# Activations in place, one squaring instruction and six early gate heads in a planned attention kernel

## The chip, the cores and the metric

The kernel runs on one core of a Trainium2 chip. Its time is the device time of one execution in microseconds (us); lower is better. The core has five engines that run their own queues in order and meet at semaphores: TensorE (PE, matrix products; its weight loads are listed as PEld), VectorE (DVE), ScalarE (ACT), GpSimd (POOL) and SyncE (SP), which here issues nearly all DMA transfers.

## The reference

The model has two layers over 4 x 256 tokens of 256 channels, all in float32: a conditioning stage, an attention, a second conditioning stage and a mixture of experts, twice. Only the attention of the first layer is touched:

```python
conv = silu(causal_conv_4_taps(x @ w_qkv))
q, k, v = split(conv)                 # 16 heads of q and k, 32 of v, 128 wide
core = chunk_gated_delta_rule(l2norm(q), l2norm(k), v, g, beta)
out = core * rsqrt(mean(core * core) + EPS) * norm_w
out = out * silu(x @ w_z)
return out @ w_out
```

The delta rule needs, for each chunk of tokens, the products of keys with keys and of keys with queries (the Gram blocks), the inverse of a unit triangular matrix made of them, and with it the new values and the outputs.

## The kernel before, in words

**Tiling.** The tokens are cut into two halves (`s` = 0, 1) of two sequences `b` of 256 tokens. One *unit* is one key head of one half, with its two value heads: 16 units in each half, 32 in all. A unit holds its 256 tokens as two chunks `n` of 128. Four units form a `Group` (line 447), which shares the inversion of the 32 x 32 diagonal blocks on VectorE (`small_inverses`, line 482: 30 steps of a multiply and a subtract, plus 32 x 32 transposes). `Rest` (line 1797) holds the other stages of a half: experts, a gated mix, and eight more experts.

**A planner sets the order.** Every step is declared as an `op` (line 194) with an engine, a cost and the buffers it reads and writes. `Tape.plan` (line 289) places the steps one by one, by how late each may start and when its engine, its buffers and its inputs are free; the constants of line 418 weigh this. It plans ten times, takes the plan that it holds for the shortest, and emits the steps in that order, which is then each engine's queue. So a change to one step's cost, to a buffer count or to a constant can move steps in every queue. All of them are issued through one wrapper, so nearly everything in the profile carries line 128, and groups are told apart by tile names.

**Places.** Every tile of 512 elements in a partition takes one of `PLACES` = 59 common places (`place`, line 1443). `MOST` caps how many places one use may hold at a time (4 if not named), and `RATE` and `FEW` keep some free for more urgent steps.

**Around the change, in one unit.** `products` (line 771) loads `wqk` and makes `acck_k` and `accq_q` (`convolved`, line 728: two products on PE, a scaled copy on ACT, three taps on DVE). ACT takes the Silu of each half of each, into `kq[0]` and `kq[1]`, which hold chunk `n` of keys (`j` = 0) and queries (`j` = 1) side by side. `gram` (line 795) multiplies a chunk's keys with the keys and queries of a chunk in one matmul of 256 columns per sequence. ACT squares each `kq` into `sq`, and `norms` (line 851) sums the squares on PE into `ps_kt`; small steps on DVE and POOL make the scales of them. POOL and ACT build the decay matrices `attnT`. `values`, `inverse` and `outputs` follow and leave the outputs in `vo[0]` and `vo[1]`. `normed` (line 1277) takes the sum of squares of each row of `vo` into `rs`: four ACT instructions for each chunk, each with an accumulator that a further instruction reads out. POOL adds an epsilon, takes the power -1/2, and scales `vo` by `rs` and by the gate `zs`; PE turns it into `oT` and `project` (line 658) multiplies by `wo`.

**Early gates.** `gates` (line 1213) is the product `x @ w_z` and its Silu: 8 float32 matmuls of 256 columns for each of two chunks. For units named in `EARLY` (line 421), which are two (heads 3 and 4 of half 0), it is declared ahead of all groups (`early`, line 1260), kept in DRAM, and loaded back when `normed` needs it. Each float32 matmul is two MATMUL instructions in the profile, each with a weight load.

Of the kernel before, what the change touches and what calls it, by code (L numbers as in the profile page):

```python
# [414 lines left out]
            o.emit()  # L415


ROUNDS, SWITCH, LOAD, SPARE, AHEAD, EACH, END, IDLE, MOMENT, GAP, RATE, GIVES = 10, 11.7, 1.3, 106.8, 160.0, 23.99, 1300.0, 54.95, 0.68, 66.3, 3.14, 5.0
UNIT = 42

EARLY, FEW = range(3, 5), 6
WIDE = 96
WINDOW, ENOUGH, LITTLE, SLOW, THIN = 3.4, 0.51, 0.38, 0.5, 10.0

# [260 lines left out]
class Unit:  # L685
# [85 lines left out]
    def products(self):  # L771
# [2 lines left out]
        gate = p.gateb[s]  # L774
        w = self.load("wqk")

        kq = self.kq = [self.buf([P, 2, 2, P], "kq0", 2), self.buf([P, 2, 2, P], "kq1", 6)]
        for j, at in ((1, 0), (0, 1)):
            acc = self.convolved(w, at, at * NH + h, "qk"[j == 0])
            for n in range(2):  # L780

                def emit(n=n, j=j, acc=acc):
                    e.scalar.activation(
                        kq[n]()[:, :, j, :], acc()[:, :, n * P : n * P + P], AF.Silu
                    )

                op("ACT", _act(256), emit, [acc], [(kq[n], {j})], table="silu")


        kqm = []  # L790
# [3 lines left out]
        cost = lambda n: (engine, length(n))  # L794
        def gram(n0, n, ps):
            for b in range(2):
                e.tensor.matmul(
                    ps()[:, b * 256 : b * 256 + 256],
                    kq[n0]()[:, b, 0, :],
                    kq[n]()[:, b].rearrange("p j d -> p (j d)"),  # L800
                    start=True,
                    stop=True,
                )

        for pairs in (((0, 0),), ((1, 1), (0, 1))):
# [11 lines left out]
            op(  # L817
                "PE",
                _mm(256, 2 * len(of)),
                grams,  # L820
                kq[: len(of)],
                [ps for _, _, ps, _ in of],
                to=[m for _, _, _, m in of],
            )
# [12 lines left out]
        sums = lambda j: ps()[:, 504 + 4 * j : 508 + 4 * j]  # L837

        sqs = []
        for n in range(2):  # L840
            sq = self.buf([P, 2, 2, P], "sq", 2, name=n)
            sqs.append(sq)
            op(
                "ACT",
                _act(512),
                lambda n=n, sq=sq: e.scalar.activation(sq(), kq[n](), AF.Square),
                [kq[n]],
                [sq],
            )

        def norms(ps=ps):


            for at in reversed(range(8)):
                j, n, b = at // 4, at // 2 % 2, at % 2
                e.tensor.matmul(
                    ps()[:, 505 + at - WIDE : 505 + at],
                    sqs[n]()[:, b, j, :],
                    p.const(LT)[:, P - WIDE :],
                    start=True,  # L860
                    stop=True,
                )
# [414 lines left out]
    def normed(self):  # L1277


        p = self.p  # L1280
        e, op = p.e, p.tape.op
        vo, zs = self.vo, self.zs
        tt = e.gpsimd.tensor_tensor
        junk = self.buf([P, P], "junko", 1)
        rs = self.buf([P, 2, 2, 2], "rs", 3)

        def o(n):
            return vo[n]().rearrange("p v b d -> p (v b) d")

        def roots(n):  # L1290
            return rs()[:, n].rearrange("p v b -> p (v b)")

        for n in range(2):

            def squares(n=n):
                for q in range(4):
                    e.scalar.activation(
                        junk(), o(n)[:, q, :], AF.Square, accum_out=roots(n)[:, q : q + 1]
                    )

            op("ACT", 1.95, squares, [vo[n]], [junk, (rs, {n})])

        def shifted():
            eps = self.eo().rearrange("p (n b) -> p n b", n=2)
            tt(rs(), rs(), _over(eps, 2, 2), ALU.add)

        def root():
            flat = rs().rearrange("p n v b -> p (n v b)")
            tt(flat, flat, p.neghalf, ALU.pow)

        op("POOL", 0.22, shifted, [self.eo], [rs])
        op("POOL", 1.64, root, [], [rs])
# [17 lines left out]
        self.oT = []  # L1330
        for v in range(2):
            oT = self.buf([P, 512], "oT", 4, name=v)
            self.oT.append(oT)
            ps = p.ps(f"ot{v}_{self.tag}")

            def turn(v=v, ps=ps):
                for b in range(2):
                    for n in range(2):
                        at = (2 * b + n) * P
                        e.tensor.transpose(  # L1340
                            ps()[:, at : at + P], vo[n]()[:, v, b, :], p.const(IDENT)
                        )
# [12 lines left out]
class Program:  # L1355
# [80 lines left out]
            return self.place(tag, name, shape)  # L1436
        return Buf(self.tape, pool, shape, tag, f"{tag}_{name}", bufs)

    PLACES = 59

    MOST = {'attnT': 20, 'kq1': 12, 'kq0': 2, 'kqm': 16, 'cross': 10, 'vo': 8, 'zs': 6, 'oT': 6, 'w0': 6, 'hw0': 8, 'w1': 6, 'hw1': 8, 'wo': 2, 'sq': 4, 'r0': 5, 'wqk': 20, 'vn': 20, 'acck': 20, 'wb0': 12}

    def place(self, use, name, shape=(P, 512)):

# [772 lines left out]
```

## Time and profile before

| what | value |
|---|---|
| median of 3 runs (lowest, highest) | 1481.29 us (1479.42, 1482.24) |
| the profiled execution's own time | 1474.44 us |
| its span, first to last instruction | 1472.6 us |
| mean granted PE clock | 0.981 of full |
| places, cap of `wqk`, `vo`, `wo`, `wb0` | 59, 20, 8, 2, 12 |
| MATMUL instructions of the early gates | 32 |
| DMA, mean rate | 87 GB/s |

The profile is of one execution. In its engine rows a percentage is busy time over the span. A row of a group has the engine, the operation, the tiles (output, then inputs), the shape, the count, then busy time in us and the mean ns of one instruction, and last the idle time of its engine just before it with what ended that. Matmuls overlap: the mean of a MATMUL is its latency from start to end, and what one costs in a row of many is the distance from start to start, which the timeline shows. In a table of stages each engine has its busy us and, in brackets, its instructions; PEclk is the granted clock.

### The profile page before, as it was taken

Reading aid. Unit: us, or ns where it says so; the run is one execution under the profiler, and the core shown is the slowest. Engines: PE = TensorE matmul, PEld = TensorE weight load, DVE = VectorE, ACT = ScalarE, POOL = GpSimd, SP = SyncE. Lnnn points to the kernel's source line nnn. Section 1 sums busy time; section 2 is a strip of 40 time slices with the busy share of each in tenths; the row PEclk is TensorE's granted clock in tenths of the full one; section 3 lists DMA queues with packets and bytes.
Section 4 is the critical chain, followed back from the end, with each engine's and each line's share of the span. In section 5 each row is a group of like instructions: output and inputs, shape, how many; then the busy total and the mean of one; then the engine's idle time right before and its main releaser. Section 6 shows DMA issues by size and latency. Waiting matters only on the chain.

```text
span 1472.6 us, 24086 instructions
## 1 busy us (share of the span) xinstructions
PE 1388.6 (94%) x8428; PEld 899.4 (61%) x8428; DVE 1127.7 (77%) x2117; ACT 932.7 (63%) x2013; POOL 918.6 (62%) x913
## 2 busy tenths in 40 slices
PE   4987899999999899999999999889999999999988
PEld 2655676876875686776687677654445644444433
DVE  7799898798698679889879989955785677785133
ACT  2688788888878888888888887733342742121220
POOL 3069859948754785985986875448643654664032
PEclk9998999999999899999999999999999999999999
DMA  6042122211120231222231223155332231658030
GB/s 213 10 136 76 47 77 87 83 46 41 59 73 29 74 98 62 66 73 72 66 110 50 65 54 94 44 165 157 107 105 83 73 126 55 188 155 245 0 115 14
DMA packets 80953, 128.60 MB, mean 87 GB/s; under 512 B 10160, under 2 KB 26288, under 8 KB 80832
## 3 DMA queue, kind: packets, MB, share of 16 engines
q1 hardware_dynamic: 79824, 125.91, 28.0%
q8 instruction: 67, 1.10, 0.3%
q10 hardware_dynamic: 1008, 1.16, 0.3%
q14 instruction: 54, 0.44, 0.1%
HBM read 121.36 MB, written 5.67 MB: 86 GB/s over the span
## 4 chain that ended last, share of the span: by engine, by line
PE 70%; DVE 15%; POOL 5%; ACT 4%; issue 3%; DMA 2%; SPq 0%; DVEq 0%; POOLq 0%; ACTq 0%
PE ps_wo L128 7%; PE ps_cvv L128 6%; PE ps_h L128 5%; PE ps_a L128 5%; PE ps_z L128 5%; PE ps_at L128 4%; PE ps_gram L128 4%; PE ps_ae L128 4%; PE ps_e L128 3%; PE ps_kt L128 3%; PE ps_cvk L128 3%; PE ps_cvq L128 3%; PE ps_vn L128 3%; DVE accv_v L128 2%; PE ps_mix L128 2%
## 5 line engine op out<-in xcount | busy, mean ns | idle before, releaser
L128 ACT ACT_TABLE_LOAD x114 | 146.3, 1283 | 21.5 <-DVE sb_xT L128 8.9
L128 DVE SCALAR_TENSOR_TENSOR accv_v<-ps_cvv,sb_convw,accv_v 128x510 f32<-128x510 f32 (+2 forms) x192 | 141.7, 742 | 7.2 <-ACT accv_v L128 2.2
L128 POOL TENSOR_TENSOR hw_h<-hw_h,r_h 128x512 f32<-128x512 f32 x64 | 85.9, 1348 | 77.7 <-DVE hw_h L128 76.1
L128 PE MATMUL ps_cvv<-ratio,wv 128*128 128x512 f32 x256 | 122.5, 609 | 2.3 <-DVE acck_k L128 1.3
L128 PE MATMUL ps_h<-ratio,w_w 128*128 128x512 f32 x256 | 117.7, 601 | 7.4 <-DMA w_w<-in_w 5.8
L128 ACT ACTIVATE r_h<-ps_h 128x512 f32<-128x512 f32 x64 | 38.2, 597 | 132.2 <-PE ps_h L128 129.4
L128 PE MATMUL ps_a<-hw_h,w_w 128*128 128x512 f32 x256 | 117.0, 595 | 1.6 <-POOL hw_h L128 1.6
L128 PE MATMUL ps_z<-wz,ratio 128*128 128x256 f32 x480 | 116.1, 390 | 0.4 <-ACT zs L128 0.4
L128 PE MATMUL ps_wo<-oT,wo 128*128 128x512 f32 x256 | 112.8, 593 | 0.8 <-ACT oT L128 0.8
L128 POOL TENSOR_TENSOR hw_e<-hw_e,r_e 128x512 f32<-128x512 f32 x32 | 41.5, 1312 | 92.1 <-ACT r_e L128 61.0
L128 PEld LDWEIGHTS ps_z<-wz,ratio 128*128 128x128 f32 x480 | 89.8, 194 | 14.2 <-issue 0.9
L128 POOL TENSOR_TENSOR vd<-vn,dc 128x512 f32<-128x512 f32 x32 | 34.1, 1064 | 98.3 <-ACT vn L128 97.8
L128 POOL TENSOR_TENSOR X<-attnT,kqm 128x512 f32<-128x512 f32 x64 | 83.6, 1314 | 12.4 <-ACT kqm L128 12.1
L128 PEld LDWEIGHTS ps_h<-ratio,w_w 128*128 128x128 f32 x256 | 48.5, 192 | 67.2 <-issue 59.8
L128 DVE TENSOR_TENSOR xs<-xs,prod 128x30 f32<-128x30 f32 (+14 forms) x240 | 81.2, 338 | 8.2
L128 PEld LDWEIGHTS ps_a<-hw_h,w_w 128*128 128x128 f32 x256 | 48.0, 190 | 61.5 <-issue 51.6
L128 ACT ACTIVATE junko<-vo 128x128 f32<-128x128 f32 x256 | 79.4, 310 | 7.3
L128 PEld LDWEIGHTS ps_wo<-oT,wo 128*128 128x128 f32 x256 | 48.1, 190 | 58.7 <-issue 53.1
L128 DVE TENSOR_TENSOR prod<-xs,Rt 128x30 f32<-128x30 f32 (+14 forms) x240 | 78.8, 328 | 6.4
L128 POOL TENSOR_TENSOR attnT<-attnT,kqm 128x512 f32<-128x512 f32 x64 | 82.6, 1303 | 1.5
L128 DVE SCALAR_TENSOR_TENSOR hw_h<-ps_h,wb_wb 128x512 f32<-128x512 f32 x64 | 43.8, 684 | 51.8 <-ACT r_h L128 39.2
L128 PE MATMUL ps_at<-vn,attnT 128*128 128x128 f32 x512 | 82.1, 276 | 0.0
(258 smaller groups left out, 3764.1 us busy)
## 6 DMA issues: line engine op xcount, KB each, us to landing
attnT<-G SPq DMA_DIRECT2D x64, 256.0 KB, 4.9
w_w<-in_w SPq DMA_DIRECT2D x64, 256.0 KB, 4.4
wb_wb<-w_rows SPq DMA_DIRECT2D x128, 128.0 KB, 3.3
wqk<-in_wqk SPq DMA_DIRECT2D x32, 256.0 KB, 2.9
wv<-in_wv SPq DMA_DIRECT2D x32, 256.0 KB, 3.6
wo<-in_wo SPq DMA_DIRECT2D x32, 256.0 KB, 3.0
qe<-G SPq DMA_DIRECT2D x32, 256.0 KB, 3.6
wz<-in_wz SPq DMA_DIRECT2D x30, 256.0 KB, 2.7
```

The source lines that it names most:

```text
L128: return self._tc.keep_in_program_order(f(*a, **k))
```

## The change

Four things are edited, and the constants with them.

1. **Keys and queries in place.** The Silu of a unit's keys is one ACT instruction over 512 elements, written over `acck_k`; that of the queries likewise over `accq_q`. The tiles `kq0` and `kq1` are gone, so the `acc` tiles live until the last Gram block and square. Keys and queries no longer lie side by side, so each Gram matmul of 256 columns becomes two of 128. The squares are taken for keys and for queries instead of for chunk 0 and chunk 1.
2. **Output squares of the second chunk.** ACT squares all of `vo[1]` in one instruction into a new tile `osq` (one place), and VectorE sums it with one `tensor_reduce`. The first chunk stays as it was.
3. **Early gates for six units.** `EARLY` is heads 2 to 7 instead of 3 and 4.
4. **Places and caps.** 61 places; `vo` 16, `wo` 6, `wqk` 8, `wb0` 3 and `wb1` 8 (it had the 4 of a use not named). Two weights of the planner move a little (`SPARE`, `IDLE`).

```diff
-ROUNDS, SWITCH, LOAD, SPARE, AHEAD, EACH, END, IDLE, MOMENT, GAP, RATE, GIVES = 10, 11.7, 1.3, 106.8, 160.0, 23.99, 1300.0, 54.95, 0.68, 66.3, 3.14, 5.0
+ROUNDS, SWITCH, LOAD, SPARE, AHEAD, EACH, END, IDLE, MOMENT, GAP, RATE, GIVES = 10, 11.7, 1.3, 102.83, 160.0, 23.99, 1300.0, 57.77, 0.68, 66.3, 3.14, 5.0
...
-EARLY, FEW = range(3, 5), 6
+EARLY, FEW = range(2, 8), 6
...
-        kq = self.kq = [self.buf([P, 2, 2, P], "kq0", 2), self.buf([P, 2, 2, P], "kq1", 6)]
+        kq = [None, None]
         for j, at in ((1, 0), (0, 1)):
-            acc = self.convolved(w, at, at * NH + h, "qk"[j == 0])
-            for n in range(2):
-
-                def emit(n=n, j=j, acc=acc):
-                    e.scalar.activation(
-                        kq[n]()[:, :, j, :], acc()[:, :, n * P : n * P + P], AF.Silu
-                    )
-
-                op("ACT", _act(256), emit, [acc], [(kq[n], {j})], table="silu")
+            acc = kq[j] = self.convolved(w, at, at * NH + h, "qk"[j == 0])
+            op(
+                "ACT",
+                _act(512),
+                lambda acc=acc: e.scalar.activation(acc(), acc(), AF.Silu),
+                [],
+                [acc],
+                table="silu",
+            )
+
+        def chunk(j, n, b):
+            return kq[j]()[:, b, n * P : n * P + P]
...
-                e.tensor.matmul(
-                    ps()[:, b * 256 : b * 256 + 256],
-                    kq[n0]()[:, b, 0, :],
-                    kq[n]()[:, b].rearrange("p j d -> p (j d)"),
-                    start=True,
-                    stop=True,
-                )
+                for j in range(2):
+                    at = (2 * b + j) * P
+                    e.tensor.matmul(
+                        ps()[:, at : at + P],
+                        chunk(0, n0, b),
+                        chunk(j, n, b),
+                        start=True,
+                        stop=True,
+                    )
...
-        for n in range(2):
-            sq = self.buf([P, 2, 2, P], "sq", 2, name=n)
+        for j in range(2):
+            sq = self.buf([P, 2, T], "sq", 2, name=j)
...
-        for n in range(2):
-
-            def squares(n=n):
-                for q in range(4):
-                    e.scalar.activation(
-                        junk(), o(n)[:, q, :], AF.Square, accum_out=roots(n)[:, q : q + 1]
-                    )
-
-            op("ACT", 1.95, squares, [vo[n]], [junk, (rs, {n})])
+        def squares():
+            for q in range(4):
+                e.scalar.activation(
+                    junk(), o(0)[:, q, :], AF.Square, accum_out=roots(0)[:, q : q + 1]
+                )
+
+        op("ACT", 1.95, squares, [vo[0]], [junk, (rs, {0})])
+        squared = self.buf([P, 4, P], "osq", 1)
+        op(
+            "ACT",
+            _act(512),
+            lambda: e.scalar.activation(squared(), o(1), AF.Square),
+            [vo[1]],
+            [squared],
+        )
+        op(
+            "DVE",
+            _dve(512),
+            lambda: e.vector.tensor_reduce(roots(1), squared(), AX.X, ALU.add),
+            [squared],
+            [(rs, {1})],
+        )
...
-    PLACES = 59
+    PLACES = 61
...
-'vo': 8, 'wo': 2, 'wqk': 20, 'wb0': 12
+'vo': 16, 'wo': 6, 'wqk': 8, 'wb0': 3, 'wb1': 8
```

The last two lines are cut to the entries that differ.

More of the change, by code (lines that the diff above doesn't have):

```diff
@@ L818, in products @@
                 "PE",
-                _mm(256, 2 * len(of)),
+                _mm(128, 4 * len(of)),
                 grams,
-                kq[: len(of)],
+                kq,
                 [ps for _, _, ps, _ in of],
@@ L845, in products @@
                 _act(512),
-                lambda n=n, sq=sq: e.scalar.activation(sq(), kq[n](), AF.Square),
-                [kq[n]],
+                lambda j=j, sq=sq: e.scalar.activation(sq(), kq[j](), AF.Square),
+                [kq[j]],
                 [sq],
@@ L857, in norms @@
                     ps()[:, 505 + at - WIDE : 505 + at],
-                    sqs[n]()[:, b, j, :],
+                    sqs[j]()[:, b, n * P : n * P + P],
                     p.const(LT)[:, P - WIDE :],
@@ L1437, in buf @@
         return Buf(self.tape, pool, shape, tag, f"{tag}_{name}", bufs)
-    PLACES = 59
-    MOST = {'attnT': 20, 'kq1': 12, 'kq0': 2, 'kqm': 16, 'cross': 10, 'vo': 8, 'zs': 6, 'oT': 6, 'w0': 6, 'hw0': 8, 'w1': 6, 'hw1': 8, 'wo': 2, 'sq': 4, 'r0': 5, 'wqk': 20, 'vn': 20, 'acck': 20, 'wb0': 12}
+    PLACES = 61
+    MOST = {'attnT': 20, 'kq1': 12, 'kq0': 2, 'kqm': 16, 'cross': 10, 'vo': 16, 'zs': 6, 'oT': 6, 'w0': 6, 'hw0': 8, 'w1': 6, 'hw1': 8, 'wo': 6, 'sq': 4, 'r0': 5, 'wqk': 8, 'vn': 20, 'acck': 20, 'wb0': 3, 'wb1': 8}
     def place(self, use, name, shape=(P, 512)):
```

## The prediction, made before the changed kernel was run

> **What bounds the kernel now.** I read the page's engine rows first, then its slices, then the chain of work that ended last:
>
> ```profile
> PE 1388.6 (94%) x8428; PEld 899.4 (61%) x8428; DVE 1127.7 (77%) x2117; ACT 932.7 (63%) x2013; POOL 918.6 (62%) x913
> ...
> PE   4987899999999899999999999889999999999988
> ...
> DVE  7799898798698679889879989955785677785133
> ...
> PE 70%; DVE 15%; POOL 5%; ACT 4%; issue 3%; DMA 2%; SPq 0%; DVEq 0%; POOLq 0%; ACTq 0%
> ```
>
> PE is busy 94% of the span and holds 70% of the chain, so PE sets the time, except where its row falls under 9. ACT, from which the change takes most, is third and holds 4%. The table of stages (start:end, length, then busy us by engine) shows where PE falls short:
>
> ```profile
> 40.00:100.00 60.00, 57.71 (x232) 37.16 (x232) 51.46 (x111) 46.53 (x86) 18.50 (x20) 0.98 0.27 89
> 100.00:200.00 100.00, 80.31 (x718) 63.45 (x717) 90.68 (x175) 83.42 (x176) 89.93 (x89) 0.90 0.19 58
> 200.00:900.00 700.00, 686.80 (x5438) 507.79 (x5437) 594.63 (x1119) 592.41 (x1355) 519.73 (x519) 0.99 0.23 68
> ```
>
> From 40 to 200 us PE idles 2.3 + 19.7 = 22.0 us, and from 100 to 200 at a clock of 0.90, so about 8 of its 80.3 busy us there are slowness. From 200 to 900 it idles 13.2 us of 700. In the chain the stretch from 98 to 186 us is almost all DVE and ACT (taps, transposes and the 30 steps of the first inversions): there PE has nothing urgent. The list of PE's waits from 80 to 200 us names the holes:
>
> ```profile
> PE ps_kt L128 <- ACT sq L128: 8.0, 1, 8.0
> PE ps_lu L128 <- DVE vo L128: 6.5, 1, 6.5
> PE ps_z L128 <- DVE eo L128: 2.5, 1, 2.5
> ```
>
> **The change part by part.** *Early gates.* These can move PE work out of the PE-bound stretch into those holes. The stages of tile `ps_z` alone (PE first) give what stands there now:
>
> ```profile
> 40.00:100.00 60.00, 3.81 (x16) 2.89 (x16) 1.19 (x2) 0.98 0.27 89
> 100.00:200.00 100.00, 18.30 (x64) 13.87 (x64) 4.63 (x8) 0.90 0.19 58
> ```
>
> 80 instructions, at 16 a unit, are five units before 200 us (two early, three in turn). With six early heads and heads 0 and 1 in turn there can be eight: three more, 48 instructions. At the start-to-start distance of a matmul of 256 columns, 0.215 us (below), that is 10.3 us, and 22.0 us of holes can hold it. The ends are 0 (the holes stand in PE's in-order queue before one late instruction, and the planner may still put nothing into them) and 10.3. I take 10.3, since a gate needs only the activations and a weight, both there from 40 us. A fuller PE should also hold its clock: ends 0 and 8 us, and I take 2, as the deepest hole's cause stays. The early Silu calls on ACT (0.6 us, two a unit) move with the gates into a stretch where ACT is busy 83% and on the chain; six of them cost up to 3.6 us there, and the in-place Silu gives back 0.39 us a unit (below) for the first eight units, 3.1: even. On SP and the DMA queue four more units mean four weight loads sooner, eight stores and eight reloads of 256 KB; a store's issue took 0.32 us, so 16 of them 5.1 us over several hundred, landing in 2.1 to 2.6 us. Four loads at the start, at the 241 GB/s of the first 20 us, could hold up the first inputs by 4.4 us; I take 0, since the loads of before (12.3 us) already stood behind them.
>
> *Gram blocks.* Three adjacent lines of PE's timeline (start, us, ...) price both shapes:
>
> ```profile
> 116.67 1.03 PE L128 MATMUL ps_gram<-kq 128*128 128x256 f32 x4
> 117.53 1.04 PE L128 MATMUL ps_vt<-sb_consts,accv_v 128*128 128x128 f32 x8
> 118.41 1.89 PE L128 MATMUL ps_z<-wz,ratio 128*128 128x256 f32 x8
> ```
>
> Four instructions of 256 columns took 117.53 - 116.67 = 0.86 us, 0.215 each; eight of 128, each with its own weights, 0.88, 0.110 each. A block of four becomes eight: +0.02 us, three a unit, 32 units: +1.9 us of PE. A rule speaks against this split: the Trainium skill, "TensorE: Matmul & The Clock Gate", Back-to-back issue gap, says that in a stream of weight load and matmul pairs the spacing is set by both, about 81 ns at 128 columns and 131 at 512. On a straight line between, 256 columns are 98 ns, and two of 128 cost 162/98 = 1.65 times as much. On the 12 x 0.215 = 2.58 us of Gram blocks a unit that would be +1.7 us, +54 us in all, and the change would end near 1525. The row is of this kernel's type, shape and weight loads, so the row decides; 54 us stays as the far end, given little weight.
>
> *Silu in place, and the squares.* The groups (busy us, mean ns):
>
> ```profile
> L128 ACT ACTIVATE junko<-vo 128x128 f32<-128x128 f32 x256 | 79.4, 310 | 7.3
> L128 ACT ACTIVATION_READ_ACCUMULATOR junko<-vo 128x1 f32 x256 | 48.1, 188 | 0.0
> L128 ACT ACTIVATE sq<-kq 128x512 f32<-128x512 f32 x64 | 37.8, 622 | 0.3
> L128 ACT ACTIVATE kq<-acck_k 128x256 f32<-128x256 f32 x64 | 24.1, 409 | 0.8 <-DVE k L128 0.7
> L128 ACT ACTIVATE accv_v<-accv_v 128x512 f32<-128x512 f32 x64 | 38.6, 626 | 1.2 <-DVE accv_v L128 0.8
> ```
>
> Silu: four of 0.41 us become two of 0.626, -0.39 us a unit, -12.5 us of ACT. Squares of the second chunk: four pairs of 0.310 + 0.188 = 1.99 us become one of 0.622, -1.37 a unit, -43.8 us. ACT falls by 56 us to about 876. PE's listed waits on ACT from 200 to 950 us add up to only some 6 us, so I put this at 0 (at most 6).
>
> *The sum on VectorE.* The nearest rows are small reductions:
>
> ```profile
> L128 DVE TENSOR_REDUCE r_route<-r_rk 128x32 f32<-128x256 f32 x2 | 0.8, 420 | 0.1
> L128 DVE TENSOR_REDUCE r_route<-r_route 128x4 f32<-128x32 f32 x4 | 0.7, 186 | 0.1
> ```
>
> (420 - 186)/224 = 1.045 ns an element, so 512 take 420 + 256 x 1.045 = 0.69 us; 32 of them 22.0 us of DVE, to 1150. Its cover is DVE's 105 us of idle from 200 to 900, which takes 27 or so of the units, 18.6 us: DVE goes from 85% to 88%. With the cover gone all 22 us would count. There is a new wait: the sum sits in DVE's queue until ACT has squared. Behind it wait the taps of later heads, whose PSUM banks PE needs. The planner orders both, so I take 0 and keep 0.5 us a unit, 16 us, as the far end. Below nothing is possible too: the pair takes 0.62 + 0.69 us where ACT alone took 1.99, so `rs` is ready some 0.5 us sooner; POOL's waits for it (44.6 us, "rs <- ACT junko") are of an engine off the path, so nothing is counted. Whether the sum also collides with POOL is open: the skill's "SBUF — State Buffer", SBUF: two separate sides, says that VectorE shuts GpSimd out of a shared port pair in a two-port mode or with two SBUF inputs, and "VectorE: DVE Perf Modes" that a `tensor_reduce` runs only in the plain mode. By the rule no collision; no run here shows it, and the rows fit, without excluding a blocked one. If it blocked, a wait of up to one POOL product (1.28 us) each would be 41 us of DVE.
>
> *Places and caps.* No `kq` tiles means two places fewer a unit held for as long as the Gram blocks wait; `osq` takes one and the pool gains two. That lets values and gates run further ahead: 0 to -10 us (half of PE's 13.2 us of idle from 200 to 900, and of the 7 us that a clock of 0.99 costs there), taken at 0. `wb0` falls to 3: the products of one expert (8 instructions of 0.43 us) take 3.4 us, and a row of weights lands 3.3 us after issue, so two in hand are enough: 0, or up to the 11.3 us that DVE waits for such rows now, once more.
>
> **The sum.** -10.3 (gates) - 2 (clock) + 1.9 (Gram) = -10.4 us, against the profiled execution's 1474.4 us: 1464.0. The median of the runs shown is 6.9 us higher, at 1481.3, so on it I forecast 1471.
>
> **Rivals.**
>
> 1. *VectorE becomes the pace from 200 to 900 us.* For it: DVE is busy 9 tenths in many slices there, holds 15% of the chain, and gets 22 us and a wait more. Against: PE's waits on DVE there are each under 2 us. If all of the 22 us land before steps that PE needs: 1481.3 - 10.3 + 1.9 + 22.0 = 1495. It decides from 8.4 us on, some 0.26 us a unit, where the gain is used up.
> 2. *The gates are only shuffled.* The holes stay, or the critical steps near 120 us slip by as much: 1481.3 + 1.9 = 1483. For it: the planner could fill these holes before with gates of heads 0 to 4 and left 22 us open. Against: four heads now stand free that waited behind their group.
> 3. *The plan gets looser everywhere*, thanks to places and a freer ACT: 1471 - 10 = 1461. For it: fewer tiles held; against: only 13 us of idle to win.
>
> **How the numbers follow.** 42% for the forecast (1464 to 1478), 15% for rival 3, 13% for rival 2, 30% for rival 1 and its like (any new order that keeps PE waiting). 0.2% is 3.0 us, about what a measurement of this kernel can tell from no change. Faster by more: 42 + 15 + 1 = 58%; within: 12%; slower: 30%. The range takes in rival 3 with 9 us to spare and ends at rival 1: 1452 to 1495.
>
> **What would show it.** Right: some 128 `ps_z` instructions before 200 us and less PE idle from 100 to 200 with a clock over 0.90; Gram rows of 128 columns, 768 in all, about 0.110 us apart; ACT near 876 us; DVE near 1150 with 32 sums of 0.69 us; PE idle from 200 to 900 still near 13 us. Wrong: as many gates as before by 200 us, sums longer than 0.8 us, DVE's share of the chain well over 15%, or PE waiting for DVE in that stretch. What would upset all of it is the order itself: a new plan in the first 200 us that starts the PE-bound stretch later than 186 us.

## The result, and the profile after

| | before | after |
|---|---|---|
| median of 5 runs each (lowest, highest), us | 1482.24 (1479.42, 1483.47) | 1495.0 (1492.25, 1496.02) |
| span of the profiled execution, us | 1472.6 | 1494.1 |
| mean granted PE clock | 0.981 | 0.974 |
| PE idle in the span, us | 84.0 | 92.2 |

The ratio is 1.0079, interval 1.0062 to 1.0096: the change costs 12.8 us where a gain of 10 was forecast. The profiles lie 21.5 us apart, more than the medians, since the profiled execution of before, 1474.4 us, was one of its quickest (of 134 timed runs of before on record two took 1474.5 us or less); why it was is part of what follows.

The page of the changed kernel, its engine rows, the slices of PE and DVE, and the shares of the chain of waits:

```profile
PE 1401.9 (94%) x8812; PEld 921.3 (62%) x8812; DVE 1151.6 (77%) x2149; ACT 922.1 (62%) x1744; POOL 913.3 (61%) x913
...
PE   3998799999999899999999999899999998999988
...
DVE  7799899799699779889889879875686686674133
...
PE 71%; DVE 12%; POOL 6%; ACT 4%; DMA 3%; issue 3%; SPq 1%; ACTq 0%; DVEq 0%; POOLq 0%
```

DVE's share of the chain fell from 15% to 12% while its busy time rose by 23.9 us, so VectorE did not become the pace. PE is busy 13.3 us longer: as estimates, 2 are the Gram blocks, and a clock of 0.974 instead of 0.981 makes 1401.9 x 0.007 = 10 of the rest. PE also idles 8.2 us more. The table of stages (start:end, length, busy us and instructions of PE, PEld, DVE, ACT, POOL, then PE's clock, DMA share, GB/s):

```profile
40.00:100.00 60.00, 55.90 (x265) 38.18 (x265) 50.02 (x96) 42.12 (x70) 18.58 (x23) 0.96 0.29 101
100.00:200.00 100.00, 82.45 (x699) 63.24 (x698) 90.24 (x170) 71.39 (x139) 79.60 (x79) 0.87 0.22 66
200.00:900.00 700.00, 687.62 (x5706) 521.07 (x5705) 602.97 (x1142) 589.53 (x1162) 515.77 (x515) 0.99 0.24 73
```

From 200 to 900 us PE idles 12.4 us, 13.2 before: nothing is lost there inside the stretch. From 40 to 200 it idles 21.6, 22.0 before: the holes are as large as they were, and the clock fell from 0.90 to 0.87. Of tile `ps_z` alone the same view has

```profile
40.00:100.00 60.00, 7.62 (x32) 5.78 (x32) 2.39 (x4) 0.96 0.29 101
100.00:200.00 100.00, 17.77 (x64) 13.68 (x64) 4.64 (x8) 0.87 0.22 66
```

96 gate instructions by 200 us; 80 before, 128 forecast. (A unit has four float32 matmuls of gates for each chunk, not the eight that the part on early gates gives; 16 instructions a unit are right.) What became late is the first group. The 32 x 32 transposes that open and close its small inverses (tiles `Rt` and `Tc`) start at 126.1 and 157.9 us, against 118.4 and 149.8 before. The rows of `Tc` give shortest, median and longest duration in ns, then the starts of the first group's and the last group's, before and after:

```profile
L128 DVE STREAM_TRANSPOSE Tc<-xs x8: 1934/1984/1993, 149.8 to 930.3; 128x1024 f32<-128x1024 f32 x8
```

```profile
L128 DVE STREAM_TRANSPOSE Tc<-xs x8: 1920/1988/1998, 157.9 to 938.6; 128x1024 f32<-128x1024 f32 x8
```

So some 8 us are lost before 160 us and are still missing at 940; the other 13 of the two spans' difference are lost after that. PE's stretch from the last `Tc` to the end, before and after:

```profile
930.27:1472.60 542.33, 515.70 (x1816) 255.40 (x1814) 334.40 (x592) 178.96 (x335) 262.18 (x257) 0.99 0.36 111
```

```profile
938.62:1494.10 555.48, 519.90 (x1812) 256.88 (x1810) 343.87 (x609) 183.40 (x308) 273.45 (x269) 0.98 0.36 105
```

With as many instructions left, PE idles 35.6 us there instead of 26.6.

The groups of the edited steps (busy us, mean ns, then idle before):

```profile
L128 ACT ACT_TABLE_LOAD x133 | 170.6, 1283 | 21.0 <-DVE ek L128 9.8 <-PE ps_z L128 4.0 <-DVE sb_xT L128 3.6
L128 ACT ACTIVATE junko<-vo 128x128 f32<-128x128 f32 x128 | 39.6, 310 | 3.8
L128 ACT ACTIVATION_READ_ACCUMULATOR junko<-vo 128x1 f32 x128 | 23.9, 187 | 0.0
L128 ACT ACTIVATE osq<-vo 128x512 f32<-128x512 f32 x32 | 20.2, 632 | 2.9 <-POOL attnT L128 2.0
L128 ACT ACTIVATE acck_k<-acck_k 128x512 f32<-128x512 f32 x32 | 20.0, 625 | 1.6 <-DVE acck_k L128 1.4
...
L128 DVE TENSOR_REDUCE rs<-osq 128x4 f32<-128x512 f32 x32 | 21.6, 676 | 5.5 <-ACT osq L128 5.4
```

Every price of the prediction is there: squares and their read-outs halved (79.4 to 39.6 and 48.1 to 23.9), sums of 0.676 us. But ACT fell by 10.6 us only, not 56. Its groups without table loads fall by 48, the new order switches ScalarE's function tables (Silu and the exponential, for instance, lie in different ones) 19 times more (114 to 133 loads of 1.283 us, +24 us), and the rest is overlap of neighbouring instructions, which busy time counts once: the groups sum to 68 us more than the busy time before, and to 55 after.

### The profile page after: what moved, and what is told of

The parts are those of the page before. It is cut to its first block, busy times and chain, and to the rows that moved or that the text cites. A ratio compares the mean times of both kernels' runs of the same rounds, so it can differ in the third digit from the quotient of the medians.

```text
span 1494.1 us, 24638 instructions
## 1 busy us (share of the span) xinstructions
PE 1401.9 (94%) x8812; PEld 921.3 (62%) x8812; DVE 1151.6 (77%) x2149; ACT 922.1 (62%) x1744; POOL 913.3 (61%) x913
## 4 chain that ended last, share of the span: by engine, by line
PE 71%; DVE 12%; POOL 6%; ACT 4%; DMA 3%; issue 3%; SPq 1%; ACTq 0%; DVEq 0%; POOLq 0%
PE ps_wo L128 6%; PE ps_cvv L128 6%; PE ps_z L128 6%; PE ps_h L128 5%; PE ps_at L128 5%; PE ps_a L128 5%; PE ps_gram L128 4%; PE ps_kt L128 4%; PE ps_cvq L128 3%; PE ps_vn L128 3%; PE ps_ae L128 3%; PE ps_cvk L128 3%; PE ps_e L128 2%; DMA w_w<-in_w 2%; PE ps_lx L128 2%
## 5 line engine op out<-in xcount | busy, mean ns | idle before, releaser
L128 PE MATMUL ps_z<-wz,ratio 128*128 128x256 f32 x416 | 99.9, 386 | 0.7 <-ACT kqm L128 0.7
L128 PEld LDWEIGHTS ps_z<-wz,ratio 128*128 128x128 f32 x416 | 76.3, 191 | 13.5 <-issue 2.2
L128 DVE SCALAR_TENSOR_TENSOR hw_h<-ps_h,wb_wb 128x512 f32<-128x512 f32 x64 | 43.8, 687 | 50.4 <-ACT r_h L128 47.2
L128 POOL TENSOR_TENSOR vo<-vo,zs 128x512 f32<-128x512 f32 x64 | 82.3, 1306 | 0.0
```

The source lines that it names most:

```text
L128: return self._tc.keep_in_program_order(f(*a, **k))
```

## The experiments

Two kinds of kernel are needed to tell prices from order. In a kernel with a **fixed order** only what a step emits is edited, not the cost or buffers that the planner sees, so that every queue stays as it was but for the edited instructions. A kernel **planned anew** has the edit declared, and the whole order may move. Ratios are to the kernel before, run beside each on the same chip. Three chips were used, and before's own median beside these runs lay between 1482.3 and 1486.2 us, so rows are compared by their ratios and not by their medians; a difference of 0.2 to 0.3% between two rows is about what their intervals can tell.

| run | kernel, edits | order | median us | ratio (interval) |
|---|---|---|---|---|
| after | the change | new | 1495.0 | 1.0079 (1.0062, 1.0096) |
| e2 | after, old squares | after's | 1491.43 | 1.0051 (1.0031, 1.0072) |
| e7 | after, mask | after's | 1491.9 | 1.0040 (1.0022, 1.0057) |
| e13 | after, mask, old squares | after's | 1486.48 | 1.0012 (1.0002, 1.0022) |
| e1 | before, Gram, sum late | before's | 1508.6 | 1.0176 (1.0146, 1.0205) |
| e6 | before, mask | before's | 1475.84 | 0.9938 (0.9917, 0.9959) |
| e8 | before, mask, Gram, sum late | before's | 1492.99 | 1.0064 (1.0041, 1.0086) |
| e9 | before, mask, Gram | before's | 1475.72 | 0.9948 (0.9928, 0.9968) |
| e10 | before, mask, sum late | before's | 1497.16 | 1.0090 (1.0065, 1.0116) |
| e11 | before, mask, sum early | before's | 1483.43 | 0.9999 (0.9984, 1.0013) |
| e3 | after, two early heads | new | 1489.89 | 1.0047 (1.0027, 1.0067) |
| e4 | before, six early heads | new | 1492.16 | 1.0061 (1.0042, 1.0081) |
| e12 | before, mask, six early heads | new | 1485.01 | 1.0018 (1.0000, 1.0037) |
| e14 | after, mask, two early heads | new | 1487.81 | 1.0023 (1.0008, 1.0038) |
| e15 | before, mask, new places and caps | new | 1502.29 | 1.0120 (1.0102, 1.0137) |
| e16 | after, mask, old places and caps | new | 1505.47 | 1.0155 (1.0128, 1.0183) |
| e17 | after, mask, old cap of `wb0`, `wb1` | new | 1498.62 | 1.0106 (1.0078, 1.0133) |
| e18 | before, mask, Silu in place, Gram | new | 1496.51 | 1.0094 (1.0068, 1.0120) |

**e1, the new operations in the old order.** Gram split, squares of the second chunk in one instruction, their sum on VectorE at the head of POOL's step `shifted`.

```diff
+                if n == 1:
+                    e.scalar.activation(self.osq, o(1), AF.Square)
+                    return
...
         def shifted():
+            e.vector.tensor_reduce(roots(1), self.osq, AX.X, ALU.add)
...
-                    kq[n]()[:, b].rearrange("p j d -> p (j d)"),
+                        kq[n]()[:, b, j, :],
```

> Keeps the old order of every queue and puts only two of the change's operations into it: Gram matmuls of 128 columns, and the second chunk's squares as one ACT instruction with their sum on VectorE, emitted just ahead of POOL's use. Order theory (the loss of 13 us comes from the new order, not from what the operations cost): within 4 us of before, since Gram adds about 2 us of PE and the sums lie beside other work. Operation theory (the 22 us of sums, or the doubled matmuls, set the pace): 8 to 22 us slower than before, and PE waits on VectorE from 200 to 900 us grow by as much.

1508.6 us, 1.0176: more than the whole change loses. So operations that were counted at +1.9 us in sum cost 26 in an order not made for them; e8 below parts this into what is theirs and what is not.

**e2, the old squares in the new order.** Accumulators on ACT as before, no sum; the step for the sum emits nothing.

```diff
-            lambda: e.scalar.activation(squared(), o(1), AF.Square),
+            lambda: [
+                e.scalar.activation(squared()[:, q, :], o(1)[:, q, :], AF.Square, accum_out=roots(1)[:, q : q + 1])
+                for q in range(4)
+            ],
...
-            lambda: e.vector.tensor_reduce(roots(1), squared(), AX.X, ALU.add),
+            lambda: None,
```

> Keeps the changed kernel's order and gives the second chunk's squares back to ACT with accumulators; VectorE sums nothing. Order theory: still 10 us or more slower than before (ratio 1.006 to 1.012), since the order is the same and ACT has 44 us more. Operation theory: the 13 us come back, within 4 us of before.

1.0051: by the ratios 0.28% (4 us) of the 0.79% comes back, though the two intervals overlap; more stays.

**e3 and e4, the early heads each way.**

```diff
-EARLY, FEW = range(2, 8), 6
+EARLY, FEW = range(3, 5), 6
```

> The changed kernel with early gates for heads 3 and 4 only, planned anew. If the six early heads cause the late start of the first group (first transposes of the inversion at 126 instead of 118 us), these fall back to about 118 us and 6 to 10 us come back. If the new order as a whole does it, the time stays 8 us or more above before, with another distribution of the loss.

e4 has the reverse line in the kernel before.

> The kernel before with early gates for heads 2 to 7, planned anew, nothing else. As I forecast it, 8 to 12 us faster than before, with 128 gate matmuls ahead of 200 us. If the early heads are the cause of the loss: 6 to 13 us slower, first transposes near 126 us. If any new plan loses: slower too, but with the first transposes near 118 us and the loss elsewhere.

e3 gains 0.32%, and its interval overlaps that of the change. Its first transposes start at 129.0 us, so the six early heads are not what makes the first group late. e4 loses 0.61% in a new plan with six early heads. Its first inverses start at 116.1 us and end at 153.4 (`Rt`, `Tc`), about where before has them. 120 gate instructions stand before 200 us, but PE has 836 instructions in all from 40 to 200 us, 947 before; and its busy time from 200 to 900 us falls to 677.5 us, so it idles 22.5 there instead of 13.2.

**e5, the kernel before once more.** No edit, one execution, of 1482.36 us.

> The kernel before, unchanged, looked at once more. In the first profile GpSimd lost the race for the shared port at 90 us (one product of 1.05 us took 3.87) and VectorE's 20 mask additions from 86 us took 7.5 us; with two operations exchanged and the order kept they took 16.4 us. If this is a race that a shift of 0.4 us decides, the same program may show either. If it follows from the edit, the additions take 7.5 us again and the first transposes start at 118 us.

Its span is 1480.6 us and its `Tc` starts at 156.4, 6.7 us later than in the first profile of the same program. What differs are 20 additions on VectorE, which put the causal mask on decay matrices of the first group. VectorE's timeline (start, us, then the group) in the first profile, then POOL's there:

```profile
86.07 7.53 DVE L128 SCALAR_TENSOR_TENSOR attnT<-attnT,nG,sb_consts 128x128 f32<-128x128 f32 x20
...
87.89 1.09 POOL L128 TENSOR_TENSOR attnT<-attnT,c 128x512 f32<-128x512 f32 x1
90.63 3.87 POOL L128 TENSOR_TENSOR attnT<-attnT,c 128x512 f32<-128x512 f32 x1 [1.65 <-ACT attnT L128]
94.46 2.53 POOL L128 TENSOR_TENSOR X<-attnT,kqm 128x512 f32<-128x512 f32 x2
```

and the same in e5:

```profile
86.63 15.46 DVE L128 SCALAR_TENSOR_TENSOR attnT<-attnT,nG,sb_consts 128x128 f32<-128x128 f32 x20
...
88.98 1.09 POOL L128 TENSOR_TENSOR attnT<-attnT,c 128x512 f32<-128x512 f32 x1
91.23 1.21 POOL L128 TENSOR_TENSOR attnT<-attnT,c 128x512 f32<-128x512 f32 x1 [1.15 <-ACT attnT L128]
92.40 2.60 POOL L128 TENSOR_TENSOR X<-attnT,kqm 128x512 f32<-128x512 f32 x2
```

In the first profile one POOL product of 1.04 us lasts 3.87, and the twenty additions take 7.53 us, 0.38 each; in e5 POOL's products last 1.2 to 1.3, and the additions take 15.46 us, 0.77 each. Each time one engine stands while the other works. The Trainium skill, "SBUF — State Buffer", SBUF: two separate sides, has the rule for this: a VectorE instruction with two inputs in SBUF and a GpSimd instruction that reads SBUF exclude each other from a shared port pair, and whichever starts first keeps it. (SBUF and PSUM are the two memories in which the kernel's tiles lie; the tiles `ps_` that PE writes are in PSUM.) These additions have two such inputs, `attnT` and the mask in `sb_consts`. So before's own time holds a race, worth 6.7 us of its first inverses.

The kernel's source provides for this: line 924 declares the additions `port=True`, every POOL step counts as such a step too (line 204), and the planner (line 317) starts none before the last has ended. But these are the plan's times; in both profiles the two run side by side all the same.

**e6 and e7, the mask in PSUM.** The mask is copied once into a PSUM tile, which leaves the additions one SBUF input.

```diff
-        tape.op("ACT", 0.3, lambda: e.scalar.copy(rows(), sums()[:, 256:384]), [sums], [rows])
+        def copied():
+            e.scalar.copy(rows(), sums()[:, 256:384])
+            if s == 0:
+                xs = self.psum.tile([P, 32, 32], F32, name="mask", tag="xs", bufs=1)
+                self.mask = xs.rearrange("p i c -> p (i c)")[:, :P]
+                e.scalar.copy(self.mask, self.const(FUTURE))
+
+        tape.op("ACT", 0.3, copied, [sums], [rows])
...
-                        to, to, negated[:, q : q + 1], mask, ALU.add, ALU.add
+                        to, to, negated[:, q : q + 1], p.mask, ALU.add, ALU.add
```

> The old order, with the mask of the first group's 32 additions copied once into the PSUM tile that the inversion uses later, so that each addition has one SBUF input. Port theory (an addition with two SBUF inputs waits for GpSimd's products): the additions take 0.28 us each, 9 us in all, and the first transposes start at 114 to 118 us in every run, and the kernel is 0 to 6 us faster than before. If the waits are not of the port: the additions keep their 12.8 us and the time stays within 3 us.

> The changed kernel's order with the same mask in PSUM. Port theory: additions 9 instead of 17.5 us, first transposes at about 118 instead of 126 us, and 6 to 9 of the 13 us lost come back (ratio to before 1.002 to 1.005). If the late start of the first group has other causes in the new order (GpSimd waiting 9.7 us for ACT's exponentials at 114 us): 0 to 3 us come back.

The additions in e6, their group, and in the timeline the twenty that met POOL's product:

```profile
L128 DVE SCALAR_TENSOR_TENSOR attnT<-attnT,nG,mask 128x128 f32<-128x128 f32 x32 | 8.5, 342 | 0.0
```

```profile
87.24 5.25 DVE L128 SCALAR_TENSOR_TENSOR attnT<-attnT,nG,mask 128x128 f32<-128x128 f32 x20
```

A mean of 342 ns, against 472 in before and 617 in after; the twenty take 5.25 us, 0.26 each, and the POOL product in their midst takes its usual time (1.04 us). Before gains 0.62%: at 0.9938 it is ahead of both kernels, and no other run but e9, below, comes level with it. After gains 0.39%. So the race costs both kernels; it does not make the difference between them, which with it out of the way is 1.0040/0.9938, 1.0% or 15 us. All kernels from here on have the mask in PSUM.

**e8 to e11, the operations one by one in the old order.** e8 is e1 with the mask, e9 the Gram split, e10 the sum late (the diffs of e1). In e11 the sum is issued right behind its square:

```diff
+                if n == 1:
+                    e.scalar.activation(osq, o(1), AF.Square)
+                    e.vector.tensor_reduce(roots(1), osq, AX.X, ALU.add)
+                    return
```

> The old order with both new operations (Gram of 128 columns, sum on VectorE) and the mask in PSUM. Order theory: with the race taken out, within 5 us of the old order with the mask in PSUM alone. Operation theory: 10 us or more slower than that, from PE's transposes of the outputs, which waited 11.3 us for GpSimd behind the sums.

> The old order with the mask in PSUM and Gram matmuls of 128 columns, nothing else. If the matmuls cost what the trace shows (0.110 against 0.215 us for half), 0 to 3 us slower than the mask alone (0.994 of before), so 0.994 to 0.997. If the doubled matmuls are what made the old order with both new operations slow: 10 us or more, a ratio of 1.001 or above.

> The old order with the mask in PSUM and the sum on VectorE, emitted just ahead of POOL's use, nothing else. If the sum is the cost: about 1.005 of before (17 us over the mask alone), with PE's transposes of the outputs waiting 10 us or more for POOL. If it is not: 0.992 to 0.996.

> The same with the sum put into VectorE's queue right after the square is issued on ACT. If the loss comes from the sum standing late in VectorE's queue, it falls: 0.994 to 1.000 of before, and POOL waits less for `rs`. If any sum on VectorE costs it, since VectorE then stands still for ACT: 1.003 or more, with VectorE waiting for ACT's `osq` by 10 us or more in all.

e8 is 1.3% (19 us) behind e6, so some 7 of e1's 26 us were the race's. The Gram split costs 0.1%, and the intervals of e6 and e9 overlap. The sum costs 1.5% late and 0.6% early, though it is the same sum with the same duration on VectorE. That e8, with both edits, is 0.26% ahead of e10, which has one of them, lies within their intervals. Where the sum's price is paid is seen in the list of waits from 200 to 950 us (total us, times, longest), in e6:

```profile
POOL rs L128 <- ACT junko L128: 38.1, 17, 5.9
PE ps_ot L128 <- POOL vo L128: 0.6, 1, 0.6
```

and in e10:

```profile
POOL rs L128 <- DVE rs L128: 63.7, 24, 6.7
PE ps_ot L128 <- POOL vo L128: 11.9, 14, 1.7
```

and in the row of the stage from 200 to 900, of e6, then of e10:

```profile
200.00:900.00 700.00, 686.43 (x5440) 507.70 (x5439) 595.30 (x1121) 592.88 (x1356) 520.38 (x521) 1.00 0.23 69
```

```profile
200.00:900.00 700.00, 675.71 (x5276) 495.93 (x5275) 594.21 (x1120) 558.71 (x1159) 508.27 (x509) 0.99 0.22 66
```

The sum stands in VectorE's queue behind whatever was put there first, POOL gets `rs` late, scales `vo` late, and PE, which meets the transposes of `vo` (`ps_ot`) in its own order, waits 11.9 us in 14 places instead of 0.6 in one. PE loses 10.7 us of work in that stretch, though ACT has 34 us less to do in it. In e11 that wait is 0.7 us in one place, and the stretch has 681.75 us of PE work. There VectorE itself stands 2.4 us in 4 places until ACT has squared (4.9 us in 6 over the whole kernel), and PE's wait for VectorE's `vo` ahead of `ps_vn` is 3.3 us in 4 places instead of 0.2 in one: the price is smaller, and part of it is seen elsewhere. In the changed kernel, planned with the sum in view, the wait is 3.8 us in 4 places.

**e12, six early heads without the race.** The diffs of e4 and e6.

> The kernel before, planned anew with six early heads, with the mask in PSUM so that the race for the port is out. As I forecast the early heads: faster than the mask alone, 0.986 to 0.990 of before. If they push needed work aside: 1.000 or more, with more than 80 gate matmuls ahead of 200 us and no less idle time of PE from 40 to 900 us.

1.0018 against 0.9938: the new plan with six early heads loses 0.8%. Two stages of e6, all tiles, then `ps_z` alone:

```profile
40.00:100.00 60.00, 58.42 (x230) 37.39 (x229) 50.35 (x112) 45.38 (x85) 17.30 (x22) 0.96 0.27 89
100.00:200.00 100.00, 81.06 (x716) 64.45 (x717) 86.67 (x172) 83.95 (x177) 88.14 (x86) 0.88 0.18 58
```

```profile
40.00:100.00 60.00, 3.81 (x16) 2.89 (x16) 1.19 (x2) 0.96 0.27 89
100.00:200.00 100.00, 15.35 (x64) 12.23 (x64) 4.53 (x8) 0.88 0.18 58
```

and of e12:

```profile
40.00:100.00 60.00, 59.30 (x248) 40.52 (x248) 50.09 (x117) 45.93 (x88) 16.94 (x22) 0.97 0.29 103
100.00:200.00 100.00, 80.79 (x697) 62.85 (x696) 84.06 (x151) 73.28 (x154) 83.59 (x84) 0.90 0.20 63
```

```profile
40.00:100.00 60.00, 7.65 (x34) 6.39 (x35) 2.37 (x4) 0.97 0.29 103
100.00:200.00 100.00, 21.55 (x88) 16.85 (x86) 6.36 (x11) 0.90 0.20 63
```

This is the test of the prediction's main term. The gates did come: 120 instructions by 200 us instead of 80 (the rows of e12 add up to 122, since an instruction across their border counts in both). But from 40 to 200 us PE has 943 instructions instead of 946, and 140.08 us of work instead of 139.48. 40 gate instructions came in and 43 others went out. The holes were not filled, and PE stands more later: it does 678.24 us from 200 to 900 instead of 686.43, and from 930 us on its wait for rows of weights (`ps_h` for `w_w`) is 10.0 us instead of 3.0. That it stands there for want of what was pushed out is likely but not shown.

**e13, the new order without race and sum.** The diffs of e2 and e6 in the changed kernel.

> The changed kernel, in its own fixed order, with the mask in PSUM and the second chunk's squares back on ScalarE's accumulators, so no sum on VectorE. If the sum alone were what is left of the loss, this comes to the mask-alone kernel, ratio 0.994 (1476 us), from 1.004 with the sum. If the new order carries a loss of its own, it stays at 1.000 or above (1482 to 1490 us). I expect 0.999, since the same step without the mask gave back 4 us of 12.

1.0012. Against e7 the sum costs 0.28% (4 us) in the changed kernel's own order, the same as between e2 and the change; the intervals meet at one end. Against e6 the rest of the change costs 0.74% (11 us), with no sum on VectorE and no race. The rows of `Tc`, of e6, then of e13:

```profile
L128 DVE STREAM_TRANSPOSE Tc<-xs x8: 1907/1977/2019, 147.2 to 930.0; 128x1024 f32<-128x1024 f32 x8
```

```profile
L128 DVE STREAM_TRANSPOSE Tc<-xs x8: 1929/1976/2012, 154.4 to 936.3; 128x1024 f32<-128x1024 f32 x8
```

7.2 us are lost at the start and some 6 of them are still missing at the last inverse; of the two spans' 11.8 us (1484.5 against 1472.7) some 5.5 are lost after it.

**e14, the changed kernel with two early heads** (the diffs of e3 and e6), planned anew.

> The changed kernel with the mask in PSUM, two early heads as before instead of six, planned anew. If the six early heads cost in the new plan what they cost in the old one (0.8%), this comes to 0.996 (1476 us) from 1.004. If it stays at 1.002 to 1.006, they are not what the changed kernel loses by, since the plan makes up for them elsewhere. I expect 0.999 to 1.004: without the mask the same step was worth nothing that its interval told from zero.

1.0023 against 1.0040 with six, the intervals overlap: what cost 0.8% in the old kernel is not visible here. Nor does the first group come earlier: its transposes start at 125.3 us, 122.0 in e7.

**e15 and e16, places and caps each way.** e15 puts them into the kernel before, with the mask.

```diff
-    PLACES = 59
+    PLACES = 61
...
-'vo': 8, 'wo': 2, 'wqk': 20, 'wb0': 12
+'vo': 16, 'wo': 6, 'wqk': 8, 'wb0': 3, 'wb1': 8
```

> The kernel before with the mask in PSUM and only the new number of places (61) and the new caps on the tiles, planned anew. The prediction took them at 0, at best -10 us: 0.994 (1476 us), or down to 0.987. If the caps are a cause of the loss, it is above 1.000 (1482 us or more). I expect 0.998 to 1.004, because the cap of wqk falls from 20 to 8 and that of wb0 from 12 to 3, which delays weights.

e16 is the reverse in the changed kernel.

> The changed kernel with the mask in PSUM and the old number of places (59) and the old caps, planned anew. If the new caps cost the changed kernel what they cost the old one (1.8%), this falls from 1.004 to about 0.990 (1472 us). If the new caps belong to the change (six early heads with more to park, Silu in place with fewer tiles), it stays at 1.004 or gets slower. I expect 1.004 or a little slower.

The old kernel planned with the new caps loses 1.8% (1.0120 against 0.9938), and the new kernel planned with the old caps loses 1.2% (1.0155 against 1.0040). So the caps are neither good nor bad; each set goes with its plan.

**e17, the cap of `wb0` alone taken back.**

```diff
-'wb0': 3, 'wb1': 8
+'wb0': 12
```

> The changed kernel with the mask in PSUM and only the caps of wb0 (3) and wb1 (8) taken back, to 12 and none, planned anew. The prediction kept 0 to 11.3 us for the cap of wb0. If PE's waits for weight rows late in the kernel (6.2 us in the changed kernel, 3.0 before) come from that cap, this gives back about 3 us, to 1.002; if the cap is a main cause, 0.996 (1476 us) or less; if it is harmless, 1.004.

PE's waits for `w_w` after 930 us fall from 5.0 (e7) to 3.3 us, as the cap would have it, and the kernel is 0.7% slower: in the new plan PE waits 9.9 us there for VectorE's `ratio` ahead of `ps_lg`, 2.2 in e7.

**e18, Silu in place and the Gram split alone**, with the old squares, heads, caps and settings, planned anew.

```diff
-                op("ACT", _act(256), emit, [acc], [(kq[n], {j})], table="silu")
...
+            op(
+                "ACT",
+                _act(512),
+                lambda acc=acc: e.scalar.activation(acc(), acc(), AF.Silu),
+                [],
+                [acc],
+                table="silu",
+            )
```

> The kernel before with the mask in PSUM and, of the change, Silu in place and the Gram split alone: old squares, old early heads, old places, caps and settings, planned anew. The prediction counted Silu in place at 0 and the split at +1.9 us, so 0.995 (1478 us). If a new plan with other work in it is by itself worth a per cent, it lands anywhere from 0.990 to 1.010; above 1.002 Silu in place, by way of the new plan, is a cause of its own.

1.0094 against 0.9948 for the split alone in the old order. What is added is cheaper on ACT and takes nothing on PE, but `Tc` first starts at 159.7 us, 12.5 later than in e6: a cheaper step came with a worse order. Silu in place with its order held fixed was not tried.

## Why the prediction was wrong, point by point

**What bounds the kernel: right.** PE sets the time before and after, and rival 1, VectorE as the pace from 200 to 900 us, did not come: PE's idle there is 12.4 us, 13.2 before. That its figure of 1495 is the measured one is chance. Nor did rival 3, a looser plan, since that idle time hardly moved.

**Early gates, -10.3 us: the step that failed.** It took PE's idle time before 200 us as room for gates. Its own lower end, and rival 2, said why not: the holes stand in an in-order queue before late instructions. In e12 the gates came nearly in the number forecast, as many other instructions went out, and the plan as a whole lost 0.8%. In the changed kernel 16 more came, not 48, PE idles 21.6 us from 40 to 200 us instead of 22.0, and by e14 against e7 the six heads are worth nothing that can be told from zero. What was wrong was to price a new plan as the old plan plus an edit.

**The order is what the larger part is lost to.** The prediction named it as what would upset everything, and gave it no term. e13 against e6 measures it, with the gates and the Gram split in it: +11 us. The sum adds 4 (e13 to e7), and the race takes off 3, since it costs before 9 us and the changed kernel 6 (e6, e7): 12 us, which is the change's ratio. Part of the order's loss can be seen. In the changed kernel ScalarE has Silu, squares and a gate's Silu of the next units ahead of the first group's exponentials (timeline of ScalarE, then of POOL):

```profile
96.75 1.28 ACT L128 ACT_TABLE_LOAD   x1
98.05 0.60 ACT L128 ACTIVATE zse<-ps_z 128x512 f32<-128x512 f32 x1
...
106.56 0.61 ACT L128 ACTIVATE sq<-accq_q 128x512 f32<-128x512 f32 x1
107.08 0.61 ACT L128 ACTIVATE accq_q<-accq_q 128x512 f32<-128x512 f32 x1
...
110.09 1.28 ACT L128 ACT_TABLE_LOAD   x1
111.39 2.44 ACT L128 ACTIVATE attnT<-attnT,nG 128x128 f32<-128x128 f32 x8
...
114.43 2.04 POOL L128 TENSOR_TENSOR attnT<-attnT,c 128x512 f32<-128x512 f32 x2 [9.73 <-ACT attnT L128]
```

From 96.75 to 111.39 us ACT works with the other table, and POOL stands idle 9.73 us for the exponential; in the first profile of before that wait was 1.68 us and ACT was back at its exponentials at 101.35. The race is in these figures: in e5 the same wait of before is 11.40 us. With the race away the pair is 6.76 (e7) and 3.16 us (e6), 3.6 of the 7 us by which the first inverses are late.

The end counts for as much. Set against e5, where before lost the race, the changed kernel's first and last `Tc` are only 1.5 and 0.5 us later, and its span is still 13.5 us longer. After the last `Tc` PE idles 35.6 us, 26.6 and 25.0 in the two profiles of before; among the new waits are 3.9 us for the weights `w_fc`, for which PE does not wait at all in before:

```profile
PE ps_e L128 <- DMA w_fc<-in_fcpj: 3.9, 2, 2.0
```

In e13 PE idles 28.8 us there, 24.5 in e6, and 2.0 of it are for `w_fc`. Why these weights come late was tried by no run.

Nor can the order's loss be shared out among heads, caps and Silu: planned alone into the old kernel they lose 0.8, 1.8 and 1.5%, together 0.7. It does not follow the table loads: e15 has 118 of them and a ratio of 1.0120, e14 136 and 1.0023. And a rival stands untested: the planner's weights (23.99, 54.95, 66.3 in line 418) and caps look like ones sought out for the old plan, so that any other plan may start behind it. No run changed these weights alone, not even the two that the change moves.

**The clock, -2 us: wrong in sign.** It followed from a fuller PE before 200 us, which did not come. That the clock fell from 0.90 to 0.87 from 100 to 200 us with PE as busy there (82.45 us against 80.31) is not explained.

**Gram blocks, +1.9 us: right.** In the changed kernel's timeline of PE each pair of instructions (one float32 matmul of 128 columns) starts 0.22 us after the pair before it, 0.11 an instruction:

```profile
54.18 0.38 PE L128 MATMUL ps_gram<-acck_k 128*128 128x128 f32 x2
54.40 0.39 PE L128 MATMUL ps_gram<-accq_q,acck_k 128*128 128x128 f32 x2
54.62 0.39 PE L128 MATMUL ps_gram<-acck_k 128*128 128x128 f32 x2
```

e9 puts the split at 0.1%, with an interval that overlaps that of e6. The estimate of +54 us from the figures of the Trainium skill's "TensorE: Matmul & The Clock Gate", Back-to-back issue gap, did not come.

**Silu and squares, 0 on the path and -56 us of ACT: the path right by itself, ACT's total wrong.** The groups of Silu and squares fell by 52.6 us of the 56 forecast (43.8 by the squares, as forecast, and 8.8 instead of 12.5 by Silu), and the plan spent 24 on 19 more table loads. A step's price holds for its own instructions, not for the switches that a new order puts between them.

**The sum, 0 with a far end of 16 us: under-priced.** Its duration (0.69 against 0.676 us) and its count were right, and no collision with POOL shows in durations of 664 to 687 ns. DVE's total (1150 against 1151.6) was right in part by luck: 4.7 us of it are additions slowed by the race (17.5 us instead of 12.8). What failed is the sentence that POOL's waits for `rs` belong to an engine off the path, so that nothing is counted. `rs` came later, not 0.5 us sooner: POOL's waits for it rose from 44.6 to 73.3 us. And POOL is off the path only as long as `vo` is scaled before PE meets its transposes. In the new order the sum cost 4 us (e13 to e7); in the old one 9 to 22 us (e11, e10), by its place in VectorE's queue alone.

**Places and caps, 0, at best -10: not to be priced alone.** e15 and e16 show 1.8% and 1.2% of loss, one with them put in, one with them taken out.

**What was missed altogether** is the race for the port pair in before, for the additions at least: the prediction asks about the port only for the new sum. The first profile's span is 8.0 us shorter than that of e5, the same program. The forecast put 6.9 us back by the median, so this did no harm to the number, but the stretch of 98 to 186 us, on which the gates' term rests, was read from one of the quickest executions, with the first inverses 6.7 us earlier than in the other.

## What to carry to other kernels

Where a planner writes the queues, an edit buys a new order: here the eight further plans came out 0.2 to 1.6% behind the kernel before, and the six of them with the mask in PSUM 0.8 to 2.2% behind the old order with it; so first price an edit with the order held fixed, and only then let the plan move. Idle time of the bounding engine before a late instruction is not room: count whether its instructions up to a given time grow, since as much can go out as was moved in. A sum that leaves one engine's accumulator for another's queue pays by its place in that queue, and the price is found by following its reader's reader to the bounding engine.

## What the runs showed of the hardware

**One program, two outcomes in one stretch.** The same twenty additions of 128 columns with two inputs in SBUF took 7.53 us in one execution and 15.46 in another, by whether GpSimd's or VectorE's instructions had to wait; with one input in PSUM, 5.25 us, and GpSimd's product kept its 1.04 us. Taking it out is worth 0.62% (0.41 to 0.83) in a kernel of 1480 us.

**A reduction was not touched by it.** 32 sums of 512 float32 from one SBUF tile lie between 664 and 687 ns in the changed kernel. By the timelines four of them ran wholly beside POOL's products (at 242.36, 555.33, 596.18 and 711.42 us) and took 0.68 to 0.69 us like the others.
